# Two mixture-of-experts passes around an attention stage: the third expert's search, the unread products and the 64-slot product change places

## The chip, the cores and the metric

The kernel runs on one core of a Trainium2 chip. The core has TensorE (PE in the profile, with PEld for its weight loads), VectorE (DVE), ScalarE (ACT), GpSimd (POOL) and SyncE (SP), which work side by side and wait for one another through semaphores. The metric is the device time of one launch in microseconds. Before the change it is 820.86 us, the median of three runs (817.55 to 821.42).

## The reference

The input is 8 x 1024 tokens of 256 numbers, all float32. Three layers follow one another, each with a residual:

```python
x = x + 0.5 * ffn(layernorm(x), gate_w, w1, w2)      # first pass
x = x + attn(layernorm(x), ...)                      # gated memory, chunks of 128 tokens
x = x + 0.5 * ffn(layernorm(x), gate_w, w1, w2)      # second pass
```

The ffn sends each token to one of 8 experts. In token order each expert keeps its first 320 tokens; the others get nothing.

```python
expert_idx = jnp.argmax(probs, axis=-1)
pos = jnp.cumsum(mask1, axis=0) - 1.0                # place in the expert's queue
expert_input = jnp.einsum('tec,td->ecd', sec_mask, tokens)
h = jax.nn.relu(jnp.einsum('ecd,edf->ecf', expert_input, w1))   # 256 -> 1024
expert_output = jnp.einsum('ecf,efd->ecd', h, w2)               # 1024 -> 256
out = jnp.einsum('tec,ecd->td', combine_weights, expert_output)
```

## The kernel before

**Stages.** `first_router` reads all tokens, computes the gate's logits and the mask of tokens per expert. `experts` makes the first pass, out of the input and into a DRAM tensor x1, which `copied` has filled with the residual. `attention` works through 8 chunks of 128 positions (8 batches each) and writes x2 and `out`; it also computes the second router's logits. `experts` then makes the second pass, out of x2 and into `out`. The instructions of `experts` and `attention` are issued in the order in which the program writes them; nothing reorders them on an engine.

**Finding an expert's tokens.** `Slots.begin(q)` (line 197) prepares a pair of experts, 2q and 2q+1. Two products count tokens along the mask ("d_ps", which reads the mask and "prev", the mask shifted by one tile), ScalarE copies the counts to "dg", a product "b_ps" sums them over the tiles, and VectorE turns that into "began" (L212). `Slots.tokens(e)` (line 215) then makes three products "r_ps" from "began" and "dg" (L222), and VectorE counts and sums them into the list of rows to read ("get") and to write ("put"). So tokens(2) needs begin(1). `gather(e)` reads 3 x 128 rows into "xg" by indirect DMA, issued by POOL (L276); `gate_of(e)` reads the gate values of the same rows (L287) from a small DRAM tensor gate_d, which `spread` writes. `center` (L300 to L302, VectorE) subtracts each row's mean, `turn` (L312) transposes the rows on TensorE.

An expert has 320 slots: two tiles of 128 and a third of 64. The third tile holds its 64 rows twice, on 128 partitions, so that each half of the partitions handles one half of the columns.

**Unread products.** `sh.idle(ps, n)` (L85) issues n matrix products whose results nobody reads. Each is recorded as two matmuls, as all float32 products here are. They stand at the start of `experts`: `keep(idle)` ahead of begin(0) (none in the first pass, three in the second), one twice inside begin(0), six ahead of `turn`, and one twice inside it. A buffer of the tag "y" (two of them) receives them, as it does "d_ps" and "py".

**The loop over experts.** For each expert: POOL gathers for expert e+2, SP loads weights for e+1, VectorE centres expert e+1. Eight groups f of products "ph" (L364) into three PSUM buffers of the tag "h" (which r_ps and b_ps also use) are followed by a relu on ScalarE (L371). Behind some groups the dictionary `searches` puts `tokens`, `begin` or `spread` calls for later experts. Then `turn` transposes expert e+1, and the second products "py" come: for slot tiles 0 and 1 eight products of 128x256 each (L385), VectorE's gating with the residual (L392) and a scatter of 128 rows of 1 KB (L395); then for the 64-slot tile sixteen products (L408), two VectorE steps on 64 partitions (L418, tile "xh") and a scatter of 128 half rows of 512 B (L421). The program makes a scatter wait for the scatter ahead of it, since all write the same DRAM tensor.

**Attention's order.** `ORDER` is a hand-written list of steps, each with a number and an offset of chunks: `wide1-2` is step `wide(1)` of the chunk two turns back. In the last turn only the steps with -2 have a chunk to work on. There, `wide1-2` (L1127) is TensorE's work ahead of a chain through ScalarE, POOL, VectorE and POOL (L1134 to L1155), and `back_turn2-2` (L1180) transposes its result, `logits1-2` (L1189 to L1205) makes the logits "dl_b" of the last rows, and `choose1-2` the mask.

Of the kernel before, what the change touches and what calls it, by code (L numbers as in the profile page):

```python
# [10 lines left out]
F32 = mybir.dt.float32  # L11
I32 = mybir.dt.int32
AF = mybir.ActivationFunctionType
ALU = mybir.AluOpType
# [4 lines left out]
P = 128  # L19
B, S, H = 8, 1024, 256  # L20
NT = B * S
NI = NT // P
D = 64
NC = S // P
# [3 lines left out]
FC = F // P  # L28
# [4 lines left out]
class Shared:  # L33
# [48 lines left out]
    def idle(self, ps, n):  # L82

        for _ in range(n):
            self.nc.tensor.matmul(ps[:, : NS * P], lhsT=self.ident, rhs=self.jrow, start=True, stop=True)  # L85
# [174 lines left out]
def experts(sh, routed, src, dst, weights, dr, name, idle=0):  # L260
# [4 lines left out]
    nc, tc = sh.nc, sh.tc  # L265
    with ExitStack() as st:
        rp = st.enter_context(tc.tile_pool(name=f"{name}_r", bufs=1))
        ep = st.enter_context(tc.tile_pool(name=f"{name}_e", bufs=2))
        pp = st.enter_context(tc.tile_pool(name=f"{name}_p", bufs=3, space=PSUM))
        slots = Slots(sh, rp, pp, dr, routed)  # L270
# [34 lines left out]
        def turn(xn, between=lambda n: None):  # L305

            xT = ep.tile([P, 2, CAP], F32, tag="xT", name="xT")
            pts = [pp.tile([P, 512], F32, tag="t", name="pt") for _ in range(2)]
            for s in range(NS):
                m = min(P, CAP - s * P)  # L310
                for c in range(2):
                    nc.tensor.transpose(  # L312
                        pts[c][:, s * P : s * P + m], xn[:m, s, c * P : (c + 1) * P], sh.ident[:m, :m]
                    )
                if s < NS - 1:
                    between(1)
            for c in range(2):
                nc.scalar.copy(xT[:, c, :], pts[c][:, :CAP])  # L318
            return xT

        def keep(n):

            if n:
                sh.idle(pp.tile([P, 512], F32, tag="y", name="idle", bufs=2), n)
# [5 lines left out]
        for e in range(2):  # L330
            slots.tokens(e)
            rows.append(gather(e))
        slots.begin(1)
        slots.tokens(2)
        slots.exps()
        keep(6)
        xT = turn(center(rows[0]), keep)
        slots.gates()

        searches = {  # L340
            (0, 0): [(slots.spread, 0)],
            (0, 2): [(slots.tokens, 3)],
            (0, 4): [(slots.begin, 2)],
            (1, 1): [(slots.tokens, 4)],
            (1, 3): [(slots.tokens, 5)],
            (1, 5): [(slots.begin, 3)],
# [3 lines left out]
        for e in range(E):  # L350
            xg, (a, b), at = rows[e], weights.at[e], xT

            if 0 < e < E - 2:
                rows.append(gather(e + 2))
                gates.append(gate_of(e + 2))
            if e + 1 < E:
                if e > 0:
                    weights.load(e + 1)
                xn = center(rows[e + 1])
            hT = ep.tile([P, FC, CAP], F32, tag="hT", name="hT")  # L360
            for f in range(FC):
                ph = pp.tile([P, 512], F32, tag="h", name="ph")
                for c in range(2):
                    nc.tensor.matmul(  # L364
                        ph[:, :CAP],
                        lhsT=a[:, c, f * P : (f + 1) * P],
                        rhs=at[:, c, :],
                        start=(c == 0),
                        stop=(c == 1),
                    )  # L370
                nc.scalar.activation(hT[:, f, :], ph[:, :CAP], AF.Relu)  # L371
                for search, n in searches.get((e, f), ()):
                    search(n)
                if (e, f) == (0, 0):
                    gates = [gate_of(0), gate_of(1)]
                    rows.append(gather(2))
                    gates.append(gate_of(2))
            if e + 1 < E:
                xT = turn(xn)
            gate = gates[e]  # L380
            xo = ep.tile([P, 2, H], F32, tag="xo", name="xo")
            for s in range(2):
                py = pp.tile([P, 512], F32, tag="y", name="py", bufs=2)
                for f in range(FC):
                    nc.tensor.matmul(  # L385
                        py[:, :H],
                        lhsT=hT[:, f, s * P : (s + 1) * P],
                        rhs=b[:, f, :],
                        start=(f == 0),
                        stop=(f == FC - 1),  # L390
                    )
                nc.vector.scalar_tensor_tensor(  # L392
                    xo[:, s, :], py[:, :H], gate[:, s : s + 1], xg[:, s, :], ALU.mult, ALU.add
                )
                nc.gpsimd.indirect_dma_start(  # L395
                    out=dst,
                    out_offset=bass.IndirectOffsetOnAxis(ap=slots.put[:, e, s : s + 1], axis=0),
                    in_=xo[:, s, :],
                    in_offset=None,
                    bounds_check=NT - 1,  # L400
                    oob_is_err=False,
                )

            py = pp.tile([P, 512], F32, tag="y", name="py", bufs=2)
            xh = ep.tile([P, P], F32, tag="xh", name="xh")
            for f in range(FC):
                for h in range(2):
                    nc.tensor.matmul(  # L408
                        py[h * D : (h + 1) * D, :P],
                        lhsT=hT[:, f, 2 * P :],  # L410
                        rhs=b[:, f, h * P : (h + 1) * P],
                        start=(f == 0),
                        stop=(f == FC - 1),
                        skip_group_check=True,
                    )
            for h in range(2):
                part = slice(h * D, (h + 1) * D)
                nc.vector.scalar_tensor_tensor(  # L418
                    xh[part], py[part, :P], gate[part, 2:3], xg[part, 2, h * P : (h + 1) * P], ALU.mult, ALU.add
                )  # L420
            nc.gpsimd.indirect_dma_start(  # L421
                out=dst_h,
                out_offset=bass.IndirectOffsetOnAxis(ap=slots.put[:, e, 2:3], axis=0),
                in_=xh,
                in_offset=None,
                bounds_check=2 * NT - 1,
                oob_is_err=False,
            )


def first_router(sh, rp, pool, src, routed):
# [66 lines left out]
def copied(sh, rows, i, dst):  # L498

    n = NI // len(rows)  # L500
    d_v = dst.rearrange("(i p) d -> p i d", p=P)
    for g in range(0, n, 4):
        sh.nc.sync.dma_start(d_v[:, i * n + g : i * n + g + 4, :], rows[i][:, g : g + 4, :])


class Memory:
# [646 lines left out]
    def add(self, c, u, n):  # L1153
        h, two = n // 2, slice(2 * (n % 2), 2 * (n % 2) + 2)
        self.nc.gpsimd.tensor_tensor(u.xo[h][:, two], u.xo[h][:, two], u.xr[h][:, two], ALU.add)  # L1155

    def store(self, c, u, h):
        queue = self.nc.scalar if c + 1 < NC else self.nc.sync
        for to in (self.x2, self.out):
            queue.dma_start(to[c, :, NP * h : NP * (h + 1), :], u.xo[h])  # L1160
# [75 lines left out]
turn3 turn1 add1-2 load1+1 back_turn0-2 turn2 clip-1 clip-1 lx1+1 turn3 turn2 ae0 back_turn1-2 ae0  # L1236
lx0+1 ae1 lo0-2 old1-1 lo1-2 back_turn0-2 back_turn1-2 ae1 old2-1 old3-1 proj0 clip-1 load0+2 gc0-1
std0-2 gc1-1 aem logits0-2 lx2+1 proj0 proj0 aem logits0-2 hq-1 lx3+1 tap0 tap1 step1-1 logits0-2
few tap2 logits0-2 norm+1 hq-1 hq-1 proj1 step0-1 xr0-1 proj1 prods cut abh1-1 wide1-2 proj1 theta
state-1 wide1-2 tap3 hh-1 proj2 rms1-2 theta tap4 hh-1 xo2-2 abh0-1 theta xn0+1 proj2 zk add2-2  # L1240
proj2 xo3-2 tap5 rh-1 add3-2 zk rows1 soft tap6 rows1 zk softplus lo2-2 pred rows0 lo3-2 pred
back_turn2-2 back_turn2-2 spread tap7 back_turn3-2 rts-1 back_turn3-2 rts-1 ds pred std1-2 tap8
logits1-2 rows0 logits1-2 by_out-1 kept lt logits1-2 ksq sq1 logits1-2 choose1-2 thm pred thm wide0-1 back
# [26 lines left out]
@with_exitstack  # L1270
def macaron(ctx, tc, i, out):
    sh = Shared(ctx, tc, i["gate_w"])
    dr = ctx.enter_context(tc.tile_pool(name="dram", bufs=1, space=DRAM))
    x1 = dr.tile([NT, H], F32, name="x1")
    x0 = i["hidden"].rearrange("b s d -> (b s) d")
    with ExitStack() as st:

        rp = st.enter_context(tc.tile_pool(name="rows", bufs=1))
        weights = Weights(tc.nc, st.enter_context(tc.tile_pool(name="f1_w", bufs=2)), i["w1"], i["w2"])
        routed = sh.Routed(rp, "a")  # L1280
        with tc.tile_pool(name="fr", bufs=2) as pool:
            rows = first_router(sh, rp, pool, x0, routed)
        for k in range(2):
            weights.load(k)
            copied(sh, rows, 2 * k, x1)
            copied(sh, rows, 2 * k + 1, x1)
        experts(sh, routed, x0, x1, weights, dr, "f1")
    x2 = dr.tile([NT, H], F32, name="x2")
    attention(sh, i, x1, x2, out)
    with ExitStack() as st:  # L1290
        weights = Weights(tc.nc, st.enter_context(tc.tile_pool(name="f2_w", bufs=2)), i["w1"], i["w2"])
        weights.load(0)
        weights.load(1)
        experts(sh, sh.second, x2, out, weights, dr, "f2", idle=3)


# [45 lines left out]
```

## Time and profile before

| | |
|---|---|
| median of 3 runs | 820.86 us (817.55 to 821.42) |
| the profiled execution's own time | 818.81 us |
| its span | 817.0 us |
| mean granted TensorE clock | 0.948 of full speed |
| busy: PE, POOL, DVE, ACT | 748.8, 471.0, 453.9, 347.1 us |
| first pass: entry about 37.6 to 56.7 us, experts to 212 | |
| attention about 217 to 632 us | |
| second pass: entry about 632 to 654.7 us, experts to 811 | |

The profile is one execution. Times count from the start of its span. A timeline row is a run of equal instructions: start, length, engine, line, what is written from what, how many, and in brackets the idle time of the engine ahead of it and what ended it. Stretch rows give each engine's busy time in a stretch, the granted TensorE clock (1.00 is full speed), the DMA engines' busy share and what they moved. Matmuls overlap, and their ends are modelled.

### The profile page before, as it was taken

What the parts mean: (1) busy time and instruction counts of PE and PEld (TensorE: products, weight loads), DVE (VectorE), ACT (ScalarE), POOL (GpSimd) and SP (SyncE); (2) the same over time, 40 slices, a digit from 0 to 9 for tenths busy, and PEclk for the clock granted to TensorE, in tenths of its full rate; (3) what the DMA queues carried; (4) which work ended last, traced back from release to release, by engine and by line L of the source; (5) the groups of instructions that cost most, each with busy time, mean ns of one, the idle gap of its engine ahead of it and who ended that gap; (6) DMA issues with size and microseconds to landing.
All of it is one profiled execution on the core that took longest, in us unless ns stands there. A gap on an engine that the chain in (4) does not pass through costs nothing. (4 is left out here: it accounts for less than half of the span.)

```text
span 817.0 us, 13755 instructions
## 1 busy us (share of the span) xinstructions
PE 748.8 (92%) x5256; PEld 544.1 (67%) x5256; DVE 453.9 (56%) x939; ACT 347.1 (42%) x738; POOL 471.0 (58%) x610
## 2 busy tenths in 40 slices
PE   7989999999478999899999999899975899999996
PEld 5657777777336585767767575666763577777775
DVE  7763332220418988788888868978743624322310
ACT  5411222222057676767676655766332122222221
POOL 6626445431234788888888878877754254444411
PEclk9989999999867999999999979999797799999999
DMA  9995445440213334433544532434425724444410
GB/s 299 370 386 166 136 145 168 151 141 16 94 51 80 111 73 125 123 117 79 181 106 155 131 104 80 91 123 99 130 74 183 245 73 139 139 145 139 152 63 18
DMA packets 110945, 110.40 MB, mean 135 GB/s; under 512 B 12384, under 2 KB 103904, under 8 KB 110880
## 3 DMA queue, kind: packets, MB, share of 16 engines
q1 hardware_dynamic: 73312, 66.50, 27.3%
q10 hardware_dynamic: 31680, 31.46, 12.3%
q0 software_dynamic: 5888, 11.57, 4.5%
q8 instruction: 41, 0.67, 0.3%
q14 instruction: 24, 0.20, 0.1%
HBM read 78.80 MB, written 30.64 MB: 134 GB/s over the span
## 5 line engine op out<-in xcount | busy, mean ns | idle before, releaser
L371 ACT ACTIVATE hT<-ph 128x320 f32<-128x320 f32 x128 | 55.9, 437 | 221.9 <-PE ph L364 221.9
L364 PE MATMUL ph<-xT,w1t 128*128 128x320 f32 x512 | 146.0, 438 | 0.9 <-ACT xT L318 0.9
L364 PEld LDWEIGHTS ph<-xT,w1t 128*128 128x128 f32 x512 | 94.7, 190 | 40.6 <-issue 2.7
L392 DVE SCALAR_TENSOR_TENSOR xo<-py,gate,xg 128x256 f32<-128x256 f32 x32 | 15.5, 484 | 186.9 <-PE py L385 186.9
L385 PE MATMUL py<-w2t,hT 128*128 128x256 f32 x512 | 114.6, 382 | 0.0
L385 PEld LDWEIGHTS py<-w2t,hT 128*128 128x128 f32 x512 | 96.1, 190 | 13.7
L287 POOL DMA_INDIRECT gate<-gate_d,get x48 | 45.3, 943 | 39.0 <-DMA gate_d<-gates 25.0
L1111 PE MATMUL pre<-wg,xT 128*128 128x256 f32 x256 | 61.6, 401 | 2.2 <-DVE m L870 2.2
L775 PE MATMUL pre<-xT,w 128*64 128x512 f32 x256 | 61.4, 603 | 0.5 <-ACT kk L807 0.5
L1111 PEld LDWEIGHTS pre<-wg,xT 128*128 128x128 f32 x256 | 50.8, 201 | 11.0 <-DVE m L870 2.7
L1155 POOL TENSOR_TENSOR xo<-xo,xr 128x512 f32<-128x512 f32 x32 | 42.9, 1353 | 20.3 <-DVE xo L1149 20.0
L395 POOL DMA_INDIRECT out<-xo,put x16 | 16.0, 1003 | 54.7 <-DVE xo L392 52.1
L395 POOL DMA_INDIRECT x<-xo,put x16 | 16.0, 1002 | 52.3 <-DVE xo L392 44.4
L678 ACT ACTIVATE xt<-xt,ln_nm,lx_t 128x256 f32<-128x256 f32 x64 | 34.4, 593 | 24.4 <-POOL ln_nm L673 24.4
L1149 DVE SCALAR_TENSOR_TENSOR xo<-tail,rs,gate 128x256 f32<-128x256 f32 x64 | 27.1, 477 | 25.2 <-DMA out<-xo 9.4
L964 DVE TENSOR_TENSOR gc<-ehd,c 128x1536 f32<-128x1536 f32 x16 | 40.0, 2539 | 0.3
L775 PEld LDWEIGHTS pre<-xT,w 128*64 128x64 f32 x256 | 15.8, 136 | 30.4 <-issue 22.4
L685 PE MATMUL pre<-ident,xt 128*128 128x128 f32 x128 | 21.0, 298 | 14.4 <-ACT xt L678 13.0
L876 POOL TENSOR_TENSOR abq<-qq,ab 128x512 f32<-128x512 f32 x16 | 32.8, 2051 | 1.8 <-DMA ab<-kept 1.8
L698 PE MATMUL pre<-xT,w 128*128 128x512 f32 x64 | 32.1, 631 | 0.0
L408 PE MATMUL py<-w2t,hT 128*64 128x128 f32 x512 | 31.5, 276 | 0.0
L276 POOL DMA_INDIRECT xg<-x,get x24 | 23.4, 973 | 13.9 <-DVE get L240 6.8
(254 smaller groups left out, 1593.4 us busy)
## 6 DMA issues: line engine op xcount, KB each, us to landing
w1t<-w_in SPq DMA_DIRECT2D x16, 1024.0 KB
w2t<-w_in SPq DMA_DIRECT2D x16, 1024.0 KB
xt<-hidden_in SPq DMA_DIRECT2D x16, 512.0 KB
x<-xt SPq DMA_DIRECT2D x16, 512.0 KB
xt<-x ACTq DMA_DIRECT2D x16, 512.0 KB
xr<-x ACTq DMA_DIRECT2D x16, 512.0 KB
x<-xo ACTq DMA_DIRECT2D x14, 512.0 KB
out<-xo ACTq DMA_DIRECT2D x14, 512.0 KB
```

The lines of the kernel that those rows point to most:

```text
L287: nc.gpsimd.indirect_dma_start(out=gate[:, s : s + 1], out_offset=None, in_=slots.gate, in_offset=bass.IndirectOffsetOnAxis(ap=slots.get[: ...
L364: nc.tensor.matmul(ph[:, :CAP], lhsT=a[:, c, f * P : (f + 1) * P], rhs=at[:, c, :], start=(c == 0), stop=(c == 1),)
L371: nc.scalar.activation(hT[:, f, :], ph[:, :CAP], AF.Relu)
L385: nc.tensor.matmul(py[:, :H], lhsT=hT[:, f, s * P : (s + 1) * P], rhs=b[:, f, :], start=(f == 0), stop=(f == FC - 1),)
L395: nc.gpsimd.indirect_dma_start(out=dst, out_offset=bass.IndirectOffsetOnAxis(ap=slots.put[:, e, s : s + 1], axis=0), in_=xo[:, s, :], in_o ...
L678: self.nc.scalar.activation(x, x, AF.Identity, bias=u.nm[:, j : j + 1], scale=u.r16[:, j : j + 1])
L698: self.nc.tensor.matmul(ps, lhsT=self.w3[:, k, 4 * D : 6 * D], rhs=u.xT[:, k, h * 512 : (h + 1) * 512], start=(k == 0), stop=(k == 1),)
L775: self.nc.tensor.matmul(ps[self.half[r], :], lhsT=self.w3[:, k, f * D : (f + 1) * D], rhs=u.xT[:, k].rearrange("h (p r t) -> h p r t", p=N ...
L876: self.nc.gpsimd.tensor_tensor(u.abq[:, n], u.kv[2], u.ab[:, n], ALU.mult)
L964: self.nc.vector.tensor_tensor(u.gc[:, layer], g.unsqueeze(2).to_broadcast([P, B, 3, D]), u.c3.rearrange("s n j -> s j n").unsqueeze(3).to ...
L1111: self.nc.tensor.matmul(ps[:, q * H : (q + 1) * H], lhsT=u.xT[:, k, j * P : (j + 1) * P], rhs=self.wg[:, k, :], start=(k == 0), stop=(k == 1),
L1155: self.nc.gpsimd.tensor_tensor(u.xo[h][:, two], u.xo[h][:, two], u.xr[h][:, two], ALU.add)
```

## The change

- Expert 2's search: `tokens(2)` leaves the entry and comes behind group 1 of expert 0's products. `tokens(3)` and `begin(2)` move from behind groups 2 and 4 to behind groups 3 and 5. The gate gathers of experts 0, 1 and 2 and the row gather of expert 2 are issued behind group 1 instead of group 0.
- Unread products: ahead of `turn` there are 13 instead of 6, and since tokens(2) no longer stands ahead of them, they follow directly on `begin(1)`. At the start of the second pass there are four instead of three.
- Attention gets a step `idle-2` behind `wide1-2`, which does something for the last chunk only: nine unread products into a buffer of the tag "pre".
- In each expert, the 64-slot tile's products, its gating and its scatter come ahead of those of slot tiles 0 and 1.

```diff
         slots.begin(1)
-        slots.tokens(2)
         slots.exps()
-        keep(6)
+        keep(13)
         xT = turn(center(rows[0]), keep)
         slots.gates()
 
         searches = {
             (0, 0): [(slots.spread, 0)],
-            (0, 2): [(slots.tokens, 3)],
-            (0, 4): [(slots.begin, 2)],
+            (0, 1): [(slots.tokens, 2)],
+            (0, 3): [(slots.tokens, 3)],
+            (0, 5): [(slots.begin, 2)],
...
-                if (e, f) == (0, 0):
+                if (e, f) == (0, 1):
                     gates = [gate_of(0), gate_of(1)]
                     rows.append(gather(2))
                     gates.append(gate_of(2))
...
             xo = ep.tile([P, 2, H], F32, tag="xo", name="xo")
-            for s in range(2):
...
             py = pp.tile([P, 512], F32, tag="y", name="py", bufs=2)
             xh = ep.tile([P, P], F32, tag="xh", name="xh")
...
+            for s in range(2):
+                py = pp.tile([P, 512], F32, tag="y", name="py", bufs=2)
+                for f in range(FC):
+                    nc.tensor.matmul(
...
+    def idle(self, c, u, _):
+
+        if c + 1 == NC:
+            self.sh.idle(self.pre(), 9)
...
-state-1 wide1-2 tap3 hh-1 proj2 rms1-2 theta tap4 hh-1 xo2-2 abh0-1 theta xn0+1 proj2 zk add2-2
+theta state-1 wide1-2 idle-2 tap3 hh-1 proj2 rms1-2 theta tap4 hh-1 xo2-2 abh0-1 theta xn0+1 proj2 zk add2-2
...
-        experts(sh, sh.second, x2, out, weights, dr, "f2", idle=3)
+        experts(sh, sh.second, x2, out, weights, dr, "f2", idle=4)
```

More of the change, by code (lines that the diff above doesn't have):

```diff
@@ L381, in experts @@
             xo = ep.tile([P, 2, H], F32, tag="xo", name="xo")
-            for s in range(2):
[L383 to L402, printed above, removed]
             py = pp.tile([P, 512], F32, tag="y", name="py", bufs=2)
@@ L428, in experts @@
             )
+            for s in range(2):
+                py = pp.tile([P, 512], F32, tag="y", name="py", bufs=2)
+                for f in range(FC):
+                    nc.tensor.matmul(
+                        py[:, :H],
+                        lhsT=hT[:, f, s * P : (s + 1) * P],
+                        rhs=b[:, f, :],
+                        start=(f == 0),
+                        stop=(f == FC - 1),
+                    )
+                nc.vector.scalar_tensor_tensor(
+                    xo[:, s, :], py[:, :H], gate[:, s : s + 1], xg[:, s, :], ALU.mult, ALU.add
+                )
+                nc.gpsimd.indirect_dma_start(
+                    out=dst,
+                    out_offset=bass.IndirectOffsetOnAxis(ap=slots.put[:, e, s : s + 1], axis=0),
+                    in_=xo[:, s, :],
+                    in_offset=None,
+                    bounds_check=NT - 1,
+                    oob_is_err=False,
+                )
 def first_router(sh, rp, pool, src, routed):
@@ L1238 @@
 std0-2 gc1-1 aem logits0-2 lx2+1 proj0 proj0 aem logits0-2 hq-1 lx3+1 tap0 tap1 step1-1 logits0-2
-few tap2 logits0-2 norm+1 hq-1 hq-1 proj1 step0-1 xr0-1 proj1 prods cut abh1-1 wide1-2 proj1 theta
-state-1 wide1-2 tap3 hh-1 proj2 rms1-2 theta tap4 hh-1 xo2-2 abh0-1 theta xn0+1 proj2 zk add2-2
+few tap2 logits0-2 norm+1 hq-1 hq-1 proj1 step0-1 xr0-1 proj1 prods cut abh1-1 wide1-2 proj1
+theta state-1 wide1-2 idle-2 tap3 hh-1 proj2 rms1-2 theta tap4 hh-1 xo2-2 abh0-1 theta xn0+1 proj2 zk add2-2
 proj2 xo3-2 tap5 rh-1 add3-2 zk rows1 soft tap6 rows1 zk softplus lo2-2 pred rows0 lo3-2 pred
```

## The prediction

> **What bounds the kernel now.** I read the page's slices of granted clock first, then the busy time per stretch with stretches of 3.413 us, then the timeline around the low slices and around the ends of the two expert passes.
>
> The page's clock row shows where TensorE is slow: at slice 2 (41 to 61 us), slices 10 to 12, and slices 30 to 32. Slices 2 and 30 to 32 hold the two entries into an expert pass.
>
> ```profile
> PEclk9989999999867999999999979999797799999999
> ```
>
> Per stretch, columns being stretch, length, busy time of PE, PEld, DVE, ACT, POOL, then granted clock, DMA share and GB/s:
>
> ```profile
> 39.20:42.62 3.41, 3.06 (x23) 2.20 (x22) 1.80 (x7) 0.55 (x2) 0.22 (x1) 1.00 1.09 386
> 42.62:46.03 3.41, 0.29 (x3) 0.21 (x3) 2.92 (x12) 0.25 (x1) 2.81 (x3) 1.00 1.05 408
> 46.03:49.44 3.41, 3.41 (x9) 2.31 (x10) 1.77 (x7) 0.00 (x0) 2.50 (x4) 0.50 1.06 362
> 49.44:52.85 3.41, 3.41 (x7) 1.86 (x6) 3.06 (x10) 0.00 (x0) 0.45 (x1) 0.50 1.08 390
> 52.85:56.27 3.41, 3.36 (x15) 1.78 (x13) 3.21 (x10) 0.08 (x1) 0.00 (x0) 1.00 1.07 383
> ```
>
> PE has 0.29 us of work in one stretch, and the next two are granted half the clock. The timeline of the first pass's entry (start, length, engine, line, operands, and in brackets the idle time with its releaser) says why and what it costs:
>
> ```profile
> 42.39 0.38 PE L209 MATMUL b_ps<-dg,before 128*128 128x1 f32 x2 [0.36 <-ACT dg L206]
> 45.42 0.42 DVE L212 TENSOR_SCALAR began<-jrow,b_ps 128x384 f32<-128x384 f32 x1
> 45.90 1.57 PE L222 MATMUL r_ps<-dg,began 64*128 64x129 f32 x6 [3.12 <-DVE began L212]
> 47.39 6.82 PE L85 MATMUL idle<-jrow,ident 128*128 128x384 f32 x12
> 54.05 0.38 PE L312 MATMUL pt<-ident,xn 128*128 128x128 f32 x2
> 56.66 1.34 PE L364 MATMUL ph<-xT,w1t 128*128 128x320 f32 x4 [0.45 <-ACT xT L318]
> ```
>
> PE stands still for 3.1 us, because its next work, expert 2's r_ps, needs "began", which VectorE reaches only after experts 0 and 1. Then the six unread products (12 records) run at half clock and end at 54. The transposes behind them are ready earlier: the centred rows were done by 52.5. From 100 to 200 us PE is busy 20.00 of every 20 us at clock 1.00, so what the first product at 56.66 gains, the pass gains. The second pass is alike:
>
> ```profile
> 619.80 1.73 PE L1127 MATMUL tail<-wo,rts 64*128 64x256 f32 x8
> 626.98 0.69 PE L1180 MATMUL tail<-ident,xo 128*128 128x128 f32 x2 [5.46 <-POOL xo L1155]
> 632.29 4.21 PE L85 MATMUL idle<-jrow,ident 128*128 128x384 f32 x6 [0.35 <-DVE dl_b L1205]
> 636.28 0.51 PE L203 MATMUL d_ps<-tri,mask_b 128*128 128x128 f32 x2
> 640.74 0.38 PE L209 MATMUL b_ps<-dg,before 128*128 128x1 f32 x2 [0.36 <-ACT dg L206]
> 652.12 0.38 PE L312 MATMUL pt<-ident,xn 128*128 128x128 f32 x2
> 654.73 1.34 PE L364 MATMUL ph<-xT,w1t 128*128 128x320 f32 x4 [0.45 <-ACT xT L318]
> ```
>
> Here PE waits 5.5 us ahead of 626.98, and the clock is 0.50 from 622.93 to 636.5, then again from 643.4 to 650.2. The end of the second pass is a chain of scatters:
>
> ```profile
> 808.91 0.98 POOL L395 DMA_INDIRECT out<-xo,put  x1 [2.47 <-DVE xo L392]
> 810.05 0.71 DVE L418 SCALAR_TENSOR_TENSOR xh<-py,gate,xg 64x128 f32<-64x128 f32 x2 [1.42 <-PE py L408]
> 812.10 0.98 POOL L421 DMA_INDIRECT out<-xh,put  x1 [2.21 <-DMA out<-xo,put]
> ```
>
> xh is ready at 810.76, but its scatter starts at 812.10: each scatter waits until the one before it has landed (2.42 us after its issue, by the chain that ended last), and 0.77 us more.
>
> **Entry of the first pass.** With tokens(2) gone, 13 unread products stand right behind b_ps and wait for nothing, so PE goes on at 42.8. At clock 1.00 eight records of this kind (34.84) took 2.75 us, the last one's latency in it: (2.75 - 0.49)/7 = 0.323 us each. 26 records take 8.4 us, to 51.2. What was a stretch without work is full, so I take clock 1.00. The first transpose moves from 54.05 to 51.2; it and the first product keep their distance of 2.61, so the product starts 2.85 us earlier. Two things must be ready. The gathered rows: the third gather of expert 0 was issued at 45.20 and landed after 6.2 us, under a DMA share of 1.05 to 1.1 that stays; centring it takes 1.0, to 52.4, and its transpose comes 1.83 behind the first, at 53.0. It is covered by 0.6 us; were it later, each us costs a us. VectorE's centring of expert 0 can begin with the landing of the first gather (42.39 + 5.9 = 48.3) since expert 2's search (47.50 to 49.43) is out of its way. tokens(2) comes back behind the second group of products: r_ps from 60.20 held the next product to 61.07, so 0.87 us on the path. Its VectorE part (1.9 us) falls behind the centring of expert 1, about 57.0 to 58.9; it holds one of three "h" buffers, which PE wants again for tokens(3) at about 59.1, and its last reading ends at 58.4: free. Net 2.85 - 0.87 = 2.0 us.
>
> The gate gathers are moved a group later in program order but nothing else lies between them on POOL, which waits for gate_d anyway (14.3 us idle). SP cannot issue gate_d before its eight copies end at 57.46 (58.71 before), so it lands at about 63 to 64.2 instead of 64.19; three gathers at 1.25 and 2.3 to land put the third gate at 68 to 69.9. The 64-slot product now asks for that one first, at 66.7 + 2.0 = 68.7. VectorE may wait 1.2 us, with xo behind it and its scatters; PE fills the other "y" buffer and needs this one at 72.2, so it costs nothing. expert 2's gather stays behind six gate gathers, as before. begin(2) one group later, and the changed count of SP loads ahead of w2t, move nothing with a reader in sight.
>
> **Entry of the second pass.** The nine unread products start at 621.5, behind the last wide1, and take 18 x 0.323 = 5.8 us, to 627.3. The transposes there could start at 626.98: 0.3 us late, but the other half of their rows only comes at 628.2, so nothing on the path. With the clock held, the half of these rows done at clock 1.00 gives the spacing: from rows ready (617.12) to the last transpose's end (619.87) is 2.75 us, so 630.95. Then POOL's r_b binds, 630.17 + 1.03 = 631.2, and dl_b comes at 631.2 instead of 632.04. Four unread products run 631.5 to 634.1, and d_ps starts there instead of 636.28: 2.2 us. Its operand prev would be ready at 633.4, so the fourth product (0.65 us) lies on the path; that is in the number. From there b_ps of begin(1) ends at 641.12 - 2.2 = 638.9, 13 products take 8.4, so the transposes come at 647.3 instead of 652.12: 4.8 us. The third gather, issued at 643.42 - 2.2, lands 5.3 to 5.9 later, at 647.1 at worst, centred by 648.1, wanted at 649.2. Less 0.86 for tokens(2): 3.9 us.
>
> Here a rule speaks against the change. The Trainium skill, "TensorE: Matmul & The Clock Gate", Part 4, says that a transpose doesn't count as activity for the clock gate, and Part 1 that one idle window of about 3.4 us halves the clock. Row first: the stretch 616.10 to 619.52 holds transposes and the small gwc products only, 1.96 us busy, and its clock and that of most of the next stretch is 1.00 (it falls at 622.93). By that row the transposes after 627.3 keep the clock until 631.5. By the rule the four products start at half clock, d_ps comes at about 635.6, and 1.5 us of the 3.9 is gone. I take the row, and keep the 1.5 for the range.
>
> **Ends of both passes.** Experts do the same PE work; only the order turns, 2.0 + 3.55 + 3.46 us instead of 3.6 + 3.46 + 1.9. So the last scatter is that of 128 rows. In the second pass its VectorE step starts at 810.05 as xh's did, takes 0.48 instead of 0.71, POOL follows after 0.28, at 810.8. The scatter ahead of it goes at 807.45, lands at 809.9, and frees POOL at 810.65: covered by 0.15 us. It lands 2.42 later, 813.2, where xh landed 2.2 after 812.10, 814.3: 1.1 us. First pass: xh's scatter went at 214.01 and took 2.3; now 211.98 + 0.48 + 0.28 = 212.74 and 2.42: 1.15 us, which attention's first loads (216.98) wait for. In the experts between, POOL's chain of a pass (6 gathers at 1.25, scatters 3.2 to 6.1 apart) has 7 us or more before the gathered rows are read.
>
> **Sum.** 2.0 + 1.15 + 3.9 + 1.1 = 8.1 us. Profiled execution: span 817.0 to 808.9, time 818.81 to 810.7. The median of the runs shown is 2.05 above the profiled one, which would give 812.8. I take the middle, 811.8.
>
> **Rivals.** (1) Half the gain: the rule above holds, or gathers land a us or two later than reckoned and the transposes wait, or attention's clock dips (0.9 or less at 380, 460, 560 us) fall otherwise. Gain 3 to 5, time 816 to 818. For it: the cover of the gathers is 0.6 to 1.1 us. Against: their landing is set by DMA traffic that doesn't change. (2) Slower: the clock is at half during the 26 products. Each then takes 0.65 us more, as 47.39 to 52.7 shows. All cold, the first pass's transposes come at 42.8 + 16.6 = 59.4 instead of 54.05, with tokens(2) 6.2 us lost; the second pass 638.9 + 16.6 = 655.5 instead of 652.12, with tokens(2) 4.3 lost; ends give 2.25 back: 8.3 us slower, 829. It decides from about 12 cold ones of 26, where the 8.1 are eaten. Against it: PE is at 1.00 when the first ones start, and they leave no gap. (3) No change: waits that I don't see, such as POOL's order in the experts, take the gain; 820.
>
> **How the numbers follow.** Full gain 0.66 (own range 808 to 815.5), half gain 0.17, no change 0.09, slower 0.08. A change under 0.5%, 4.1 us, is about what a measurement of this kernel cannot tell from none (before: 817.55 to 821.42). Half of the second case is still faster by that bound, the other half and nearly all of the third are the same: 0.75 faster, 0.16 same, 0.09 slower. The range goes from 806.5 (the lowest run shown, 817.55, less 8.1 is 809.5; some 3 us more where attention's dips fall well) to 818, the end of the half gain; what lies above is no change and slower, 0.17.
>
> **What would show it.** Clock 1.00 from 39 to 60 us and from 604 on through 656; the first product about 2.85 us earlier in the first pass, and in the second 28.4 us behind the end of the last wide1 (621.53) instead of 33.2; no PE gap behind r_ps of tokens(2); the end of the last product to the end of the span 1.1 us shorter. Wrong if the 13 products take more than 9 us, if L312 still waits for VectorE behind them, or if PE waits inside an expert.

## The result, and the profile after

The changed kernel takes 812.04 us (median of 6 runs, 806.79 to 814.27) beside 821.14 us before on the same chip (817.55 to 823.48): ratio 0.988, interval 0.984 to 0.992, that is 9 us faster. The forecast was 811.8. The profiled execution of after took 806.79 us, with a span of 805.0 (before: 818.81 and 817.0), so it lies 5 us under its own median, and the stretches below have to be read with that in mind. This comparison and the three experiments are four sets of executions. In two of them the kernel before takes 819 to 821 us; in the other two, on two chips other than that of experiment 2, it takes 833 to 835, and there everything turns out differently (experiments 1 and 3). A ratio leaves out executions over 1.5% above the fastest of their kernel, so it can differ from that of the medians.

The span, cut at the same events in both traces:

| stretch | before | after | change | forecast |
|---|---|---|---|---|
| start to the first d_ps | 37.65 | 38.31 | +0.66 | 0 |
| d_ps to the first product ph, pass 1 | 19.01 | 15.99 | -3.02 | -2.85 |
| experts, pass 1 | 155.28 | 155.76 | +0.48 | +0.87 |
| last product to attention's first load | 5.04 | 3.94 | -1.10 | -1.15 |
| attention, to the start of the last wide1 | 402.82 | 398.17 | -4.65 | 0 |
| last wide1 to d_ps of pass 2 | 16.48 | 16.29 | -0.19 | -2.2 |
| d_ps to the first ph, pass 2 | 18.45 | 15.66 | -2.79 | -2.6 |
| experts, pass 2 | 155.28 | 155.15 | -0.13 | +0.86 |
| last product to the end | 7.03 | 5.75 | -1.28 | -1.1 |

Without the start and attention, which the change doesn't touch, the sum is -8.0, and the forecast's is -8.2. The two agree because one missing gain (the tail, 2.0) is made up by others: 1.4 in the experts, 0.4 in the entries, 0.1 at the ends. To that extent the agreement is luck.

The page's clock row of after:

```profile
PEclk9999999999879999999999999999998999999999
```

The low digit at slice 2 is gone, and in place of the two 7s at slices 30 and 31 there is one 8 at slice 30. (The prediction read the low slices as 30 to 32; slice 32 of before is a 9, and it left out the 7s at 23 and 28, which lie in attention.) The stretches of the first pass's entry, after (stretch, length, busy time of PE, PEld, DVE, ACT, POOL, granted clock, DMA share, GB/s):

```profile
42.62:46.03 3.41, 3.06 (x11) 2.00 (x12) 3.07 (x14) 0.79 (x2) 2.45 (x3) 1.00 1.06 409
46.03:49.44 3.41, 3.41 (x13) 1.95 (x12) 0.83 (x4) 0.00 (x0) 2.60 (x3) 1.00 1.09 369
49.44:52.85 3.41, 3.41 (x15) 2.12 (x14) 2.09 (x7) 0.00 (x0) 0.95 (x1) 1.00 1.05 375
```

PE has 3.06 us of work in the stretch that held 0.29 before, and the next two run at 1.00 instead of 0.50. The timeline of after at both entries (start, length, engine, line, operands, in brackets the idle time ahead):

```profile
43.22 8.63 PE L85 MATMUL idle<-jrow,ident 128*128 128x384 f32 x26
...
52.20 0.43 DVE L300 BATCH_NORM_STATS2 ln<-xg 128x6 f32<-128x256 f32 x1 [0.74 <-DMA xg<-hidden_in,get]
53.51 0.20 PEld L312 LDWEIGHTS pt<-ident,xn 64*128 64x128 f32 x2 [0.54 <-DVE xn L302]
54.30 1.34 PE L364 MATMUL ph<-xT,w1t 128*128 128x320 f32 x4 [0.45 <-ACT xT L318]
...
612.17 2.53 PE L1127 MATMUL tail<-wo,rts 64*128 64x256 f32 x8
614.64 8.05 PE L85 MATMUL pre<-jrow,ident 128*128 128x384 f32 x18
622.52 1.04 PE L1185 MATMUL tail<-ident,xo 128*128 128x128 f32 x8
...
628.46 0.39 PE L203 MATMUL d_ps<-tri,mask_b 128*128 128x128 f32 x2
633.04 8.63 PE L85 MATMUL idle<-jrow,ident 128*128 128x384 f32 x26
...
644.12 1.34 PE L364 MATMUL ph<-xT,w1t 128*128 128x320 f32 x4 [0.45 <-ACT xT L318]
```

Both groups of 26 records take 8.63, as at full clock. Behind the first, VectorE waits for the third gathered tile (52.20), and the last transposes wait for VectorE (53.51). The tail is another matter: wide1 took 1.73 us before and takes 2.53 here, and the nine products (18 records) take 8.05 instead of the 5.8 of the forecast. They start cold, and the transposes come at 622.52, 10.35 behind the start of wide1 (before: 7.18). The stretches there:

```profile
609.05:612.47 3.42, 2.41 (x24) 1.42 (x25) 0.83 (x3) 1.34 (x3) 2.19 (x7) 0.91 1.05 361
612.47:615.88 3.41, 3.41 (x10) 2.20 (x10) 0.12 (x1) 1.44 (x7) 0.00 (x0) 0.50 0.26 87
615.88:619.29 3.41, 3.41 (x7) 1.74 (x6) 1.49 (x4) 0.46 (x2) 1.74 (x3) 0.59 0.00 0
```

The clock falls at 611.83, just ahead of wide1, behind 3.4 us in which PE is busy for 1.94 with transposes and small products. So the nine products restore the clock, where they should have kept it.

In expert 0 of the first pass a small wait has appeared (timeline of after):

```profile
72.54 0.71 DVE L397 SCALAR_TENSOR_TENSOR xh<-py,gate,xg 64x128 f32<-64x128 f32 x2 [7.63 <-DMA gate<-gate_d,get]
73.31 2.86 PE L411 MATMUL py<-w2t,hT 128*128 128x256 f32 x12 [0.35 <-DVE xh L397]
```

VectorE waits for the third gate gather, issued at 66.99, and PE behind it 0.35 us. The end of the second pass, after:

```profile
799.31 0.48 DVE L418 SCALAR_TENSOR_TENSOR xo<-py,gate,xg 128x256 f32<-128x256 f32 x1 [2.97 <-PE py L411]
800.07 0.98 POOL L421 DMA_INDIRECT out<-xo,put  x1 [2.47 <-DVE xo L418]
```

From the last VectorE step's start to the last scatter it is 0.76 us; it was 2.05 with the scatter of xh behind another.

### The profile page after: what moved, and what is told of

The parts are those of the page before. It is cut to its first block, busy times and chain, and to the rows that moved or that the text cites. A ratio compares the mean times of both kernels' runs of the same rounds, so it can differ in the third digit from the quotient of the medians.

```text
span 805.0 us, 13850 instructions
## 1 busy us (share of the span) xinstructions
PE 746.9 (93%) x5304; PEld 544.0 (68%) x5304; DVE 454.3 (56%) x939; ACT 347.1 (43%) x738; POOL 470.8 (58%) x610
## 5 line engine op out<-in xcount | busy, mean ns | idle before, releaser
L397 DVE SCALAR_TENSOR_TENSOR xh<-py,gate,xg 64x128 f32<-64x128 f32 x32 | 11.2, 350 | 114.9 <-PE py L387 107.0
L1111 PE MATMUL pre<-wg,xT 128*128 128x256 f32 x256 | 57.9, 383 | 2.9 <-DVE m L870 2.7
L1111 PEld LDWEIGHTS pre<-wg,xT 128*128 128x128 f32 x256 | 47.8, 190 | 10.9 <-DVE m L870 3.2
L876 POOL TENSOR_TENSOR abq<-qq,ab 128x512 f32<-128x512 f32 x16 | 34.6, 2163 | 2.1 <-DMA ab<-kept 2.1
L85 PE MATMUL idle<-jrow,ident 128*128 128x384 f32 x88 | 31.1, 492 | 0.4 <-DVE dl_b L1210 0.4
```

The lines of the kernel that those rows point to most:

```text
L876: self.nc.gpsimd.tensor_tensor(u.abq[:, n], u.kv[2], u.ab[:, n], ALU.mult)
L1111: self.nc.tensor.matmul(ps[:, q * H : (q + 1) * H], lhsT=u.xT[:, k, j * P : (j + 1) * P], rhs=self.wg[:, k, :], start=(k == 0), stop=(k == 1),
```

## Experiment 1: single parts

Four kernels on one chip, where the kernel before takes 832.98 us. **Entry alone** (on before):

```diff
-        slots.tokens(2)
         slots.exps()
-        keep(6)
+        keep(13)
...
+            (0, 1): [(slots.tokens, 2)],
+            (0, 3): [(slots.tokens, 3)],
+            (0, 5): [(slots.begin, 2)],
...
-                if (e, f) == (0, 0):
+                if (e, f) == (0, 1):
```

> Only the search of expert 2 behind group 1 and 13 unread products behind begin(1); slots, end of attention and the products at the start of the second pass as before. Theory (full clock and no gap make the gain, a moved search costs about 1.0): first d_ps to first product 16.0 us in the first pass (19.0 before) and 15.7 in the second (18.5 before); first product to the last product's end 156.3 in both (155.3 before); the distances behind the last product unchanged (5.0 to attention's first load, 7.0 to the end). Together about 3.8 us faster. Rival (the 26 products run cold): entries of 24 and 22 us, about 10 us slower.

Measured: 828.05 us, ratio 0.994 (0.991 to 0.997). The entries are 16.05 and 15.66 us, as in the whole change.

**Order alone**: the 64-slot tile's block ahead of the loop over the two others, on before.

> Only the 64-slot product, its gating and its scatter ahead of the other two tiles. As predicted (ends alone): 1.1 us less behind the last product in each pass, first product to last product's end 155.3 as before, together 2.2 us faster. Theory formed from the changed kernel's trace (one exposed weight load less per expert, 0.2 us each): first product to last product's end 154.0 in each pass as well, together 4.9 us faster.

Measured: 837.12 us, ratio 1.003 (1.0005 to 1.006), slightly slower. Yet experts 3 to 6 take 18.32 us instead of 18.51, expert 7 17.78 instead of 17.69, and the exits 3.93 and 5.75 instead of 5.04 and 7.03: 1.1 + 1.3 at the ends and about 1.1 per pass inside are there. They are lost in the first two experts of pass 1: 31.0 and 26.0 us, where the next kernel, with the old order, has 27.4 and 23.0 on the same chip.

**Tail alone**: the step with nine products and four instead of three at the start of the second pass, on before.

> Only the nine unread products behind the last wide1 and four instead of three at the start of the second pass. From the start of the last wide1 to the second pass's first d_ps it was 16.5 us before. As predicted (clock held): 14.3 us. Rival (the clock falls while transposes and small products run, ahead of the nine): 16 us or more, and nothing or a loss in the time; the nine products take 8 us instead of 5.8.

Measured: 831.98 us, ratio 0.997 (0.994 to 0.9997): at best 1 us. The last wide1 takes 2.49, the nine products 8.12, wide1 to d_ps 16.32.

**Without the 13 products** (on after):

```diff
-        keep(13)
+        keep(0)
```

> The changed kernel without any unread product between begin(1) and the transposes (two passes). Theory (they are there for the clock): TensorE stands still for some 7 us in both entries, the transposes start with the gathered rows, about 1 to 1.5 us earlier than in the changed kernel, but the first products run at half clock for 3.4 to 7 us and lose 1.7 to 3.4 us in each pass: 1 to 4 us slower than the changed kernel. Rival (the moved search alone gives the gain): as fast as the changed kernel, or up to 2 us faster.

Measured: 834.14 us, ratio 1.000 (0.997 to 1.003); entries 16.20 and 15.18, about as long as with them. It is taken up in experiment 3.

**What holds expert 0 on this chip.** Each of these kernels spends 27 to 33 us in expert 0 of pass 1, where the first two executions shown need 21.0 (before) and 22.6 (after). Timeline of the tail-alone kernel (old order of tiles):

```profile
72.97 0.48 DVE L392 SCALAR_TENSOR_TENSOR xo<-py,gate,xg 128x256 f32<-128x256 f32 x1 [7.70 <-PE py L385]
78.21 0.27 PE L408 MATMUL py<-w2t,hT 128*64 128x128 f32 x1 [1.02 <-issue]
79.62 0.37 PE L408 MATMUL py<-w2t,hT 128*64 128x128 f32 x1 [1.13 <-issue]
81.01 0.37 PE L408 MATMUL py<-w2t,hT 128*64 128x128 f32 x1 [1.02 <-issue]
82.41 1.84 PE L408 MATMUL py<-w2t,hT 128*64 128x128 f32 x10 [1.03 <-issue]
83.19 0.48 DVE L392 SCALAR_TENSOR_TENSOR xo<-py,gate,xg 128x256 f32<-128x256 f32 x1 [9.74 <-remote]
```

and of the order-alone kernel:

```profile
81.08 0.71 DVE L396 SCALAR_TENSOR_TENSOR xh<-py,gate,xg 64x128 f32<-64x128 f32 x2 [16.32 <-remote]
81.85 5.62 PE L410 MATMUL py<-w2t,hT 128*128 128x256 f32 x16 [7.96 <-DVE xh L396]
```

Something ends at about 81 to 83 us in both. ("remote" means that the trace names no engine or DMA as the releaser. On these chips the traces hold no landing of any gather, so when a gate came is inferred from VectorE's start.) The gate issued first seems to be there ahead of it: the old order's VectorE goes on at 72.97, a "y" buffer comes free, and PE works on until about 77. The new order wants the gate issued third and goes on only at 81.08; both "y" buffers are full, and PE stands still for 8 us. Then its eight products (16 records) take 5.62 us instead of the 3.72 of a full clock: the trace has the half clock from 78.9 to 85.7.

## Experiment 2: the late gate and the tail

Four kernels on a chip where the kernel before takes 819.31 us: the whole change, and the change with one thing altered. **The change itself:**

> The changed kernel itself, beside the three others of this set. If the chip is like the one of the first comparison (the kernel before near 821): ratio 0.985 to 0.992. If it is like the one of the four single parts (before near 833, the gate gathers of the first pass landing near 82 us): expert 0 of pass 1 takes over 30 us, and the ratio is 0.993 to 1.0, since the order with the 64-slot tile first loses there what the entry gains.

Measured: 811.13 us, ratio 0.9915 (0.989 to 0.994), the first case; expert 0 of pass 1 takes 22.99 us.

**Without the nine products** (`idle-2` out of the order):

> The change without the nine products behind the last wide1; the rest is the change. If the transposes keep the clock (the row that the prediction took), the stretch from the last wide1's start to d_ps is 2 us longer than in the whole change. If they don't (the rule), the nine products win nothing, since they themselves run at half clock: the stretch stays within 0.7 us of the whole change's 16.3, and so does the time.

Measured: 814.28 us, ratio 0.993 (0.991 to 0.995); wide1 to d_ps 17.65 us beside 16.25 with them. The clock is down at wide1 in both, and the nine still save 1.4 us, so the second guess ("they win nothing") fails too. In the whole change on this chip wide1 takes 2.52 and the nine 8.03, as in the first execution shown. Timelines of the kernel without the nine, and of the next kernel (gates turned), each from the last wide1:

```profile
617.24 2.55 PE L1127 MATMUL tail<-wo,rts 64*128 64x256 f32 x8
625.18 0.69 PE L1185 MATMUL tail<-ident,xo 128*128 128x128 f32 x2 [5.40 <-POOL xo L1155]
634.89 0.39 PE L203 MATMUL d_ps<-tri,mask_b 128*128 128x128 f32 x2
```

```profile
612.95 1.73 PE L1127 MATMUL tail<-wo,rts 64*128 64x256 f32 x8
614.61 6.07 PE L85 MATMUL pre<-jrow,ident 128*128 128x384 f32 x18
620.52 0.38 PE L1185 MATMUL tail<-ident,xo 128*128 128x128 f32 x2
627.32 0.38 PE L203 MATMUL d_ps<-tri,mask_b 128*128 128x128 f32 x2
```

In the second the clock holds, the nine take 6.07, and d_ps comes 14.37 behind wide1: 2.1 under the 16.48 of before, the 2.2 of the forecast to a tenth. The steps from the transposes ahead of wide1 to the nine products are the same as in the whole change.

**Gates turned** (third slot's gate issued first, on after):

```diff
-            for s in range(NS):
+            for s in (2, 0, 1):
                 nc.gpsimd.indirect_dma_start(
                     out=gate[:, s : s + 1],
```

> The change with one thing turned: each expert's three gate gathers are issued in the order third, first, second, as the products with the 64-slot tile first read them. Theory (the late third gate is what this order loses in expert 0 of pass 1): on a chip where the gates land in time, PE's 0.35 us wait ahead of the second tile's products goes; where they land near 82 us, the wait shrinks by the distance of two gathers at most (2.5 us), if the gathers land one after the other. Rival (all the gates land together, behind other transfers): expert 0 stays as long as in the whole change, within 0.5 us.

Measured: 811.9 us, ratio 0.991 (0.988 to 0.994). Expert 0 of pass 1 takes 21.95 instead of 22.99, VectorE's first step no longer waits for a gate, and PE runs through:

```profile
68.80 7.17 PE L411 MATMUL py<-w2t,hT 128*128 128x256 f32 x32
68.92 0.71 DVE L397 SCALAR_TENSOR_TENSOR xh<-py,gate,xg 64x128 f32<-64x128 f32 x2 [4.45 <-PE py L387]
```

The mechanism is there, 1.04 us here; it is too small to be seen in the times.

**Attention's constants later** (on after; the loads are held back to expert 3 by clears on POOL):

```diff
+                if late and e == 3:
+                    late()
...
+            nc.gpsimd.memset(t[..., 0:1], 0.0)
             nc.sync.dma_start(t, src)
```

> The change with the attention's constant loads (some 28 small ones on SP's queue at 68 to 87 us) issued at expert 3 of pass 1 instead, held there by a clear of each buffer on POOL. Theory (the gate gathers wait behind these loads in the DMA engines): the gates land within 6 us of their issue, expert 0 of pass 1 takes about 22 us, expert 1 about 21.8: on a slow-gate chip 8 to 12 us faster than the whole change, on a chip like the first within 1 us of it, with PE's 0.35 us wait gone. Rival (the gates are late by themselves or behind the weight loads): no change in expert 0.

Measured: 813.17 us, ratio 0.991 (0.989 to 0.994); expert 0 of pass 1 takes 21.94. The third gate, issued at 66.56, is used at 70.50 (issued 67.06, used 72.48 in the change itself). So the small loads do cost the gates about 1.5 us on this chip. Whether they are to blame on the other kind of chip is answered below.

## Experiment 3: the count of unread products, and a combination

Four kernels on a chip where the kernel before takes 835.07 us.

> The changed kernel once more, as the measure for the three others of this set. d_ps to first product 16.06 us in pass 1 and 15.66 in pass 2, as in its other executions. If the gates land in time (expert 0 of pass 1 near 22.5 us): ratio 0.985 to 0.993.

Measured: 836.73 us, ratio 0.999 (0.997 to 1.002). Here the whole change wins nothing.

**Without the 13 products**, again, and **with six of them** (`keep(6)` in after):

> The change without any of the 13 products (only the two single ones between the transposes stay), now beside the whole change. Theory: once expert 2's search is behind the experts' first products, the gathered rows set the entry, and the 13 products only keep the clock: the first product comes within 0.6 us of the whole change's time (even 0.4 us earlier in pass 2), but TensorE, after 6.5 us without work, runs its first products at half clock, so expert 0 is 1.3 to 2 us longer in each pass: 2 to 3.5 us slower in all. Rival (the products are what the entry gains by, as my prediction counted it): 5 us or more slower.

> The change with six products behind begin(1), as many as the old place had, instead of 13. Theory of place (a gap of some 3 us is too short to cost the clock for long): within 1 us of the whole change, the first product up to 0.5 us earlier. Rival (any gap of over 2 us ahead of the transposes halves the clock, as in the kernel before): 1.5 us or more lost in expert 0 of each pass, as without any product.

Measured: 837.14 us without (ratio 1.002, 0.9995 to 1.004), 838.80 with six (1.000, 0.995 to 1.004). Over the executions that the ratios count, the medians are 837.1 without, 834.6 with six and 835.0 with 13. The intervals overlap, so the expected loss of 2 to 3.5 us without any product is neither shown nor excluded. The entries are 16.27 and 15.18 us without, 16.07 and 14.91 with six, 15.98 and 15.66 with 13. With the same six products but tokens(2) still ahead of them they were 18.15 and 18.12 (order alone) and 18.35 and 18.52 (tail alone). Timeline of the kernel without them, first pass:

```profile
49.57 0.69 PE L312 MATMUL pt<-ident,xn 128*128 128x128 f32 x2 [6.55 <-DVE xn L302]
...
53.29 0.47 PE L312 MATMUL pt<-ident,xn 64*128 64x64 f32 x2
54.17 1.34 PE L364 MATMUL ph<-xT,w1t 128*128 128x320 f32 x4 [0.41 <-ACT xT L318]
```

The clock does fall in the gap of 6.55 us (half clock from 46.9 to 53.8), and the first transposes are cold. But they start 11.7 us behind d_ps instead of 13.4, the last ones wait for the third gathered tile anyway, and by the first product (1.34 us) the clock is back. So it is in three of the four entries recorded without the products. In the fourth (experiment 1, pass 1) the half clock goes on to 57.9, 3.8 us past the first product, whose first four records take 2.50; at half speed for 3.8 us, an estimated 1.9 us are lost there. With 13, no entry recorded shows the half clock. What moved the entry is tokens(2), not the count; the products guard the clock of the first products, and are needed for it only at times.

**A combination**: gates turned, constants late, 12 products instead of 13, three instead of four ahead of d_ps.

```diff
-        keep(13)
+        keep(12)
...
-            for s in range(NS):
+            for s in (2, 0, 1):
...
-        experts(sh, sh.second, x2, out, weights, dr, "f2", idle=4)
+        experts(sh, sh.second, x2, out, weights, dr, "f2", idle=3)
```

> The change, with the gate gathers of an expert issued third slot first, the attention's constant loads held back to expert 3, 12 products instead of 13 in both entries, and three instead of four ahead of the second d_ps. From the runs so far: 0.5 to 1.0 us of the late gate, 0.45 + 0.65 us of the 13th product, 0.65 us of the fourth: 2 to 2.7 us below the whole change, more where the gates land late. If the products were needed to hold the clock to the last, it is no faster.

Measured: 827.93 us, ratio 0.992 (0.989 to 0.995) where the whole change stands at 0.999: it beats both kernels here. (On the other kind of chip it wasn't run.) Entries 15.51 and 15.05, wide1 to d_ps 14.49: the clock fell 2.6 us ahead of wide1 and was back during the nine, which take 6.94, and one product less stands ahead of d_ps. The largest part is in the first two experts of pass 1: 24.0 and 27.4 us, where the change with six products has 34.6 and 25.4. Timeline:

```profile
72.88 0.71 DVE L399 SCALAR_TENSOR_TENSOR xh<-py,gate,xg 64x128 f32<-64x128 f32 x2 [9.07 <-PE py L413]
73.65 3.72 PE L413 MATMUL py<-w2t,hT 128*128 128x256 f32 x16 [1.79 <-DVE xh L399]
79.23 0.43 PE L366 MATMUL ph<-xT,w1t 128*128 128x320 f32 x1 [0.51 <-issue]
79.94 0.80 PE L366 MATMUL ph<-xT,w1t 128*128 128x320 f32 x2 [0.28 <-issue]
...
82.76 0.72 PE L222 MATMUL r_ps<-dg,began 64*128 64x129 f32 x5 [1.13 <-issue]
82.83 0.88 DVE L420 SCALAR_TENSOR_TENSOR xo<-py,gate,xg 128x256 f32<-128x256 f32 x2 [9.23 <-remote]
83.07 0.77 ACT L373 ACTIVATE hT<-ph 128x320 f32<-128x320 f32 x2 [16.03 <-remote]
```

VectorE goes on at 72.88 again, as in the tail-alone kernel, now with the gate wanted first. The rest still ends at 82.8, though none of attention's constants is issued before 83 us: they are not what holds these chips up, and that part of the theory of experiment 2 falls. The gain therefore fits the gates' order; as four edits stand in this kernel, the split between them is argued, not measured one by one.

## Why the prediction was right, and where not

- **Entry 1, the product 2.85 us earlier**: right (d_ps to product -3.02, clock 1.00, the 26 records 8.63 against 8.4). But the mechanism was half of it. The prediction credited 13 products at full clock; without any of them the entry is about as long. The gain is that VectorE and PE no longer pass through tokens(2) ahead of the transposes. The gathered rows, which it called covered by 0.6 us, are the bound that takes over: the last transposes wait 0.54 us for VectorE. That is one of its own signs of being wrong. Rival 2 (cold products) did not come true.
- **tokens(2) behind group 1, 0.87**: 0.96 net in expert 0 (20.98 to 21.94 in pass 2, where no gate is late); if the new order saves 0.19 there, as in the experts behind it, about 1.15.
- **The gate's lateness "costs nothing"**: wrong, by its size. It put gate_d at 63 to 64.2 and the third gate at 68 to 69.9 (its own terms give 67.8 to 69.0); gate_d came at 64.49 and the gate at about 72.4, because that gather took 5.4 us and not the 2.3 that the term used. That was the median: the trace of before has gate gathers of 2.2 to 5.3 us between 60 and 80 us. Expert 0 of pass 1 lost 0.6 to 1.05 us, PE waiting inside it, which is another of its signs of being wrong. On two chips it lost several.
- **Tail, d_ps 2.2 earlier, by the row**: this term failed. The Trainium skill ("TensorE: Matmul & The Clock Gate", Part 4, with Part 1) was weighed against one row of before, in which transposes kept the clock, and the row was taken. In the 14 profiled executions of this case the last wide1 took 1.73 us three times (before, gates turned, constants late) and 2.49 to 2.67 eleven times, with the same transposes ahead of it. The rule fits the usual case, though the fall came earlier than where the prediction applied it; the row was the rarer draw.

  The row of -0.19 in the table sets the rare draw of before beside the usual one of after. Among executions in which wide1 ran slow, wide1 to d_ps takes 16.96 and 17.20 us without the nine and with three products ahead of d_ps (order alone, entry alone), and 16.25 to 16.63 with the nine and four. So the step wins 0.3 to 0.95 us in the usual draw and 2.1 in the rare one.

  Why the clock holds at times is open. In each trace the half clock begins and ends on a grid of 3.413 us: every stretch of it lasts a whole multiple (3.41, 6.83, 10.24, 13.65, 17.07 or 20.48 us), but for the last, which runs into the trace's end. The grid lies elsewhere in each execution. In the last whole step of the grid ahead of wide1, PE is busy 2.0 to 2.1 us in the three executions that held the clock through wide1 and 1.94 to 1.96 in eight of those that lost it, so a small shift of the grid may decide. Busy time alone does not: one execution (the change in experiment 3) lost it behind 2.19 us.
- **Entry 2, 4.8 less 2.2**: right (-2.79), with the same remark on the count of products. Measured from the end of the last wide1, the first product comes 29.4 us later, where the forecast had 28.4 and before 33.2.
- **Experts "do the same PE work"**: short. The new order makes each expert from 1 to 6 0.19 us shorter (expert 7 is 0.09 longer), and the order alone does so too. The rows suggest why: before, PE's weight loads stood idle at two changes between 64 and 128 columns, after at one. Groups of one expert before:

```profile
155.32 1.73 PEld L408 LDWEIGHTS py<-w2t,hT 128*64 128x64 f32 x32 [0.33 <-issue]
157.22 8.37 PEld L364 LDWEIGHTS ph<-xT,w1t 128*128 128x128 f32 x32 [0.17 <-issue]
```

  and after:

```profile
166.96 3.10 PEld L411 LDWEIGHTS py<-w2t,hT 128*128 128x128 f32 x15 [0.17 <-issue]
```

  It gives about 1.1 us per pass over experts 1 to 7, and filled the hole that the tail left.
- **Ends, 1.15 and 1.1**: right (1.10 and 1.28).
- **Attention "untouched"**: its 4.65 us in the profiled execution are clock dips that fell otherwise. In attention the traces have the half clock for 54.6 us before and 34.5 in this execution; in its execution of experiment 2 the same kernel has 55.0 us of it and takes 403.68. The middle between the two forecasts, from the profiled execution and from the median, came within 0.3 us of the measured median; with runs 6 to 7.5 us apart that closeness is luck.
- **"No change" as a rival**: given a tenth, for waits that it didn't see. On the two chips with the hold-up in the first experts the ratio is 0.999 for the whole change (one of the two; on the other only its parts were run), through waits of that kind. The forecast held for the kind of chip on which the profile was taken.

## What to carry to other kernels

Turning the order in which an engine reads several gathered values means turning the order of the gathers too: the one wanted first must be issued first, as the slack is that of the slowest landing and not of the median one. A granted clock read in one execution near a lightly loaded stretch is one draw; look at the same place in several executions before it carries a term of a sum. Filler that keeps the clock pays only if the work behind it has its data by then: run the kernel without it before giving it credit. And before a row of before is set beside one of after, look whether the clock was in the same state in both.

## What the runs showed of the hardware

On the two chips of experiments 1 and 3 PE, ACT and VectorE are held up together in the first two experts of both passes, most in pass 1: PE's rows come at a pace of 0.70 us (79.23, 79.94) or 1.40 us (78.21, 79.62, 81.01, 82.41) with no wait named, ACT and VectorE do nothing, the DMA engines' busy share is 0.02 from 77 to 80 us in the combination, and all three are back within 0.3 us (82.76, 82.83, 83.07). POOL issues its run of gathers 1.25 us apart meanwhile, until 79. It isn't the constants' loads, and no load of instructions falls in it either: in the combination's trace they come at 63.9 and 87.1. What it is, the traces don't say, and it stays open. The kernel before has no trace on these chips, but the tail-alone kernel, whose experts are the same, spends 97.4 us in its first two experts over both passes, where before has 85.8 in its trace. These 11.6 us fit the difference of its times, 833 against 821, and they decide there whether this change is worth anything.
